# First attention: probabilities turned in place by VectorE in 32x32 blocks, values on every partition group, product in 32x32 tiles

## The chip, the cores and the metric

The kernel runs on one core of one Trainium2 chip. The core has five engines with instruction streams of their own: TensorE (matrix products; PE in the profile, its weight loads PEld), VectorE (DVE), ScalarE (ACT), GpSimd (POOL) and SyncE (SP), which here issues most of the DMAs. The metric is the device time of one execution in microseconds (us); lower is better.

## The reference, cut to what matters

There are 8 sequences (batches) of 128 tokens with 512 features, all in 32-bit floats. A transformer block is computed in two halves:

```python
x = x + attn1(einsum('bsi,boi->bso', x, lora_weight[adapter]))   # the first attention
x = x + ffn(attn2(x))                                            # the second stage
# attn1: 32 query heads of 16 features, 8 key/value heads, each shared by 4 query heads
scores = einsum('bihd,bjhd->bhij', q, k) * 16 ** -0.5
scores = where(causal, scores, finfo.min)
attn = softmax(scores)                     # [b, 32 heads, 128 queries, 128 keys]
out = einsum('bhij,bjhd->bihd', attn, v)   # then out @ wo
```

The change is in `attn1`, in the step from `attn` to `out`. The second stage (an attention over a paged cache with 32 heads of 128 features, its projections and a feed-forward layer with LoRA terms) is not touched.

## The kernel before

Everything is issued by hand in one order; each engine works through its own instructions in that order, and semaphores make it wait for the others.

The first attention fills roughly the first 205 us of the span, and the merging of LoRA weights runs beside its end. Its main loop runs over steps `k = 0..16`. Steps `2b` and `2b+1` belong to batch `b`; `hb = k % 2` selects half of its 32 heads, namely 16 heads, which lie as 4 row groups `j` of 32 partitions, 2 query repeats `rr` and 2 halves `half` (a head has 16 features, so that two heads share the 32 rows of a group, and zeros fill the other half). Step 16 has only left-over work. A step does the following:

- `scores1(k)` (L574 on): TensorE adds the causal mask (16 bf16 products in tiles of 32 rows, L583) and the scores (8 products of 32 rows by 256 columns, L595) into two PSUM tiles `sc` of 8 heads each. VectorE takes the negated maxima `nm` (L604), two instructions.
- `exps1(k, n)` (L613): ScalarE computes 8 exponentials for each of the two PSUM tiles, into an SBUF tile `pr` of 128 queries x 8 heads x 128 keys.
- `divide1(k, n)` (L623): VectorE sums (L627) and takes reciprocals (L628), GpSimd multiplies (L629).
- In the step after, `flip_p(last, j, copy)` (L633), for the four groups `j`: TensorE turns four 128x128 blocks of `pr` against the identity (L638), and VectorE or ScalarE copies the result from PSUM to an SBUF tile `pT` (L644). Keys then lie on the partitions.
- At the end of that step, `values1(last)` (L649): 8 products, 128 keys by 32 rows of output each (L657), and one copy by VectorE into `oT` (L664).

Beside this a step does its share of the projections of the next batch. An even step holds `flip_x1` (a finished batch turned for the second stage, x1Tp, L499), `condition(b+1)` (the LoRA layer, hp, L514, copied to `hT` by VectorE), `project_k` and `project_v` (kvp, L545 and L552), `keep_k` and `keep_v` (L556, L563; ScalarE copies; the values go to `vpad`, which has the zeros). An odd step holds `out_proj1(b-1)` (att, L673, added to the input by VectorE as `x1`, L677, and written to DRAM by SP), `project_q(b+1)` (qp, L530, copied to `qT` by VectorE, L540), `flip_x(b+2)` (xTp, L499) and `load_x`. The next even step's scores need `qT`.

Some steps hold extra work. Step 1 ends with `indices` (four VectorE instructions for `idx_kv`), steps 3 and 5 with `tables` (GpSimd), steps 3 and 7 issue the loads of second-stage weights on SP, step 9 issues `merge_loads` on SP (its last ones, `las` and `lbs`, wait for buffers that `condition(7)` frees in step 12). Step 12 ends with `merge_gates` (five VectorE instructions), step 13 with the gathers `kg` and `vg` (GpSimd), step 14 has `merge_a` (four products aeff and four VectorE copies `a_eff`, L464), step 15 has the first query and key products of the second stage with `q_turn`, `kv_turn` and `norms` (VectorE, ScalarE and GpSimd in turn), step 16 `queries(0)`, `merge_b` (beff) and `merge_w` (weff). After the loop come `keys(0)`, `own_keys(0)` and two more `merge_w`.

PSUM has three pools of two buffers each. `tp` serves everything that is turned, `mm` the projections and, before, the value products, `sc` the scores. In SBUF, `pr` has four buffers and `pT` five.

The second stage turns its own probabilities by VectorE in 32x32 blocks (L883) and moves the blocks by DMA; it is mentioned here since its rows in the profile show that instruction.

## Time and profile before

| | |
|---|---|
| median of 3 runs | 1414.29 us (1413.98 to 1414.86) |
| the profiled execution's own time | 1423.96 us |
| its span (first to last instruction) | 1421.1 us, mean granted TensorE clock 0.997 |
| TensorE (PE) busy | 1391.5 us, 98% of the span |
| VectorE (DVE) busy | 931.8 us, 66% |
| ScalarE (ACT) busy | 655.9 us, 46% |
| GpSimd (POOL) busy | 568.2 us, 40% |

The profile is of one execution. The page has the busy time of each engine, the groups of instructions by line with their count, busy time and mean duration, and the chain of waits that ended last. The trace behind it answers for stretches of the span: windows with the busy time of each engine, and a timeline in order of time. A line of the timeline has the start, the time taken, the engine, the line of the kernel, the operation, the tiles (out<-in), the shapes and how many instructions are merged; a bracket at its end tells how long the engine had been idle before it and which instruction ended that. A 32-bit matrix product appears as two records (two passes over its columns), one that turns a block or works in bf16 as one. Ends of matrix products are modelled, so the distance between starts is the better measure of what one costs.

In the windows one batch of the first attention in the middle takes 21.8 us.

### The profile page before, as it was taken

What the parts mean: (1) busy time and instruction counts of PE and PEld (TensorE: products, weight loads), DVE (VectorE), ACT (ScalarE), POOL (GpSimd) and SP (SyncE); (2) the same over time, 40 slices, a digit from 0 to 9 for tenths busy, and PEclk for the clock granted to TensorE, in tenths of its full rate; (3) what the DMA queues carried; (4) which work ended last, traced back from release to release, by engine and by line L of the source; (5) the groups of instructions that cost most, each with busy time, mean ns of one, the idle gap of its engine ahead of it and who ended that gap; (6) DMA issues with size and microseconds to landing.
All of it is one profiled execution on the core that took longest, in us unless ns stands there. A gap on an engine that the chain in (4) does not pass through costs nothing.

```text
span 1421.1 us, 20290 instructions
## 1 busy us (share of the span) xinstructions
PE 1391.5 (98%) x6244; PEld 898.5 (63%) x6244; DVE 931.8 (66%) x2266; ACT 655.9 (46%) x1520; POOL 568.2 (40%) x553
## 2 busy tenths in 40 slices
PE   6999989999999999999999999999999999999998
PEld 6877755566666666666666666666666665666555
DVE  5777846566666666666666666666666665666651
ACT  3555535444444444444444444444444444344431
POOL 5774342433333333333333333333333433343220
PEclk9999999999999999999999999999999999999999
DMA  6255013444444565444445654444456544444440
GB/s 198 75 164 183 31 37 104 129 117 118 119 115 119 161 193 151 119 119 119 119 119 159 196 148 119 118 119 119 121 160 192 152 117 136 131 111 112 115 111 30
DMA packets 156202, 180.26 MB, mean 127 GB/s; under 512 B 92416, under 2 KB 97792, under 8 KB 156096
## 3 DMA queue, kind: packets, MB, share of 16 engines
q1 hardware_dynamic: 140544, 134.39, 34.0%
q0 software_dynamic: 15552, 44.58, 10.8%
q8 instruction: 50, 0.82, 0.2%
q14 instruction: 56, 0.46, 0.1%
HBM read 75.83 MB, written 4.72 MB: 57 GB/s over the span
## 4 chain that ended last, share of the span: by engine, by line
PE 93%; DVE 2%; issue 2%; DMA 1%; ACT 1%; POOL 1%; SPq 1%; another core or an unknown queue 0%; DVEq 0%; POOLq 0%; ACTq 0%
PE op L963 19%; PE qp L177 15%; PE sc L889 15%; PE yp L982 15%; PE kvp L217 7%; PE sc L896 4%; PE fp L1044 2%; PE hp L514 2%; PE qTp L254 2%; PE pT1p L638 2%; PE qp L530 2%; PE att L673 2%; PE o L657 1%; PE sc L595 1%; PE kvp L545 1%
## 5 line engine op out<-in xcount | busy, mean ns | idle before, releaser
L902 DVE CUSTOM_DVE_ANT_0 pr<-sc,mask,nq 128x640 f32<-128x640 f32 x256 | 226.0, 884 | 144.2 <-PE sc L896 90.9
L912 ACT ACTIVATE pr<-pr,nm 128x640 f32<-128x640 f32 x256 | 211.8, 827 | 189.3 <-DVE nm L902 102.1
L889 PE MATMUL sc<-kT,qT 128*128 128x512 f32 x512 | 262.0, 593 | 0.0
L177 PE MATMUL qp<-wq,x1T 128*128 128x512 f32 x512 | 251.2, 593 | 0.0
L963 PE MATMUL op<-pT,vg 128*128 128x256 f32 x1024 | 242.0, 379 | 1.6 <-DMA pT<-fl 1.6
L203 POOL TENSOR_TENSOR qa<-qa,qb 128x512 f32<-128x512 f32 x64 | 81.8, 1278 | 375.2 <-DVE sums L879 375.2
L982 PE MATMUL yp<-wo,oT 128*128 128x512 f32 x504 | 229.2, 598 | 2.0 <-DVE oT L971 2.0
L963 PEld LDWEIGHTS op<-pT,vg 128*128 128x128 f32 x1024 | 193.9, 190 | 27.8 <-DVE sums L879 1.8
L880 ACT ACTIVATE pr<-pr,sums 128x640 f32<-128x640 f32 x256 | 208.4, 814 | 0.0
L883 DVE STREAM_TRANSPOSE fl<-pr 128x640 f32<-128x640 f32 x252 | 189.2, 808 | 0.0
L896 PEld LDWEIGHTS sc<-kTo,qT 128*128 128x128 f32 x512 | 96.4, 190 | 124.4 <-issue 119.2
L982 PEld LDWEIGHTS yp<-wo,oT 128*128 128x128 f32 x504 | 91.4, 191 | 95.1 <-issue 91.5
L160 POOL DMA_INDIRECT kg<-in_k_cache_dram,idx_kv x128 | 131.6, 1029 | 35.3 <-issue 34.8
L160 POOL DMA_INDIRECT vg<-in_v_cache_dram,idx_kv x128 | 128.6, 1005 | 37.8 <-issue 33.6
L889 PEld LDWEIGHTS sc<-kT,qT 128*128 128x128 f32 x512 | 87.7, 191 | 80.2 <-issue 77.8
L256 ACT COPY qT<-qTp 128x512 f32<-128x512 f32 x64 | 37.5, 586 | 205.3 <-PE qTp L254 204.7
L217 PEld LDWEIGHTS kvp<-wkv,x1T 128*128 128x128 f32 x512 | 97.3, 190 | 40.5 <-issue 30.1
L217 PE MATMUL kvp<-wkv,x1T 128*128 128x256 f32 x512 | 121.0, 379 | 0.0
L244 POOL TENSOR_TENSOR rs<-ss,minus_half 128x5 f32<-128x5 f32 x64 | 76.5, 1196 | 83.1 <-DVE ss L242 82.2
L177 PEld LDWEIGHTS qp<-wq,x1T 128*128 128x128 f32 x512 | 82.8, 191 | 31.5 <-issue 31.5
L896 PE MATMUL sc<-kTo,qT 128*128 128x128 f32 x512 | 99.2, 275 | 0.0
L273 ACT COPY kTo<-kTp 128x128 f32<-128x128 f32 x64 | 17.1, 267 | 166.4 <-issue 115.2
(155 smaller groups left out, 1701.1 us busy)
## 6 DMA issues: line engine op xcount, KB each, us to landing
pT<-fl SPq DMA_DIRECT2D x1008, 80.0 KB
kT<-flk SPq DMA_DIRECT2D x480, 32.0 KB
wq<-in_wq_dram SPq DMA_DIRECT2D x8, 1024.0 KB
wo<-in_wo_dram SPq DMA_DIRECT2D x8, 1024.0 KB
wkv<-in_wkv_dram SPq DMA_DIRECT2D x8, 512.0 KB
kg<-in_k_cache_dram,idx_kv POOLq DMA_INDIRECT x128
vg<-in_v_cache_dram,idx_kv POOLq DMA_INDIRECT x128
res<-x_kept SPq DMA_DIRECT2D x8, 256.0 KB
```

Source lines behind the costliest of these rows:

```text
L160: nc.gpsimd.indirect_dma_start(out=dst[:, c].rearrange("p n d -> p (n d)"), out_offset=None, in_=src, in_offset=bass.IndirectOffsetOnAxis( ...
L177: nc.tensor.matmul(s["qp"][:].rearrange("p h d -> p (h d)"), x1T[b][:, c, :], weights[g][0][:, c, :], start=(c == 0), stop=(c == KC - 1),)
L203: nc.gpsimd.tensor_tensor(qa[:], qa[:], qb[:], ALU.add)
L217: nc.tensor.matmul(s["kp"][:], x1T[b][:, c, :], weights[g][1][:, c, :], start=(c == 0), stop=(c == KC - 1))
L880: nc.scalar.activation(prs[r][:], prs[r][:], AF.Copy, scale=sums[:, r : r + 1])
L883: nc.vector.transpose(s["flips"][:, :, :, r, :].rearrange("p b c j -> p c b j"), prs[r][:])
L889: nc.tensor.matmul(sc[:, : NBLK * P].rearrange("p (k j) -> p k j", j=32), s["qT"][:, r, :], s["kT"], start=True, stop=True,)
L896: nc.tensor.matmul(sc[:, NBLK * P : NK], s["qT"][:, r, :], s["kTo"][:], start=True, stop=True)
L902: nc.vector.tensor_tensor_reduce(out=pr[:], in0=sc[:, :NK], in1=mask[:], scale=s["nq"][:, r : r + 1], scalar=3.0e38, op0=ALU.add, op1=ALU.min,
L912: nc.scalar.activation(pr[:], pr[:], AF.Exp, bias=nm[:, r : r + 1], scale=-1.0, accum_out=sums[:, r : r + 1],)
L963: nc.tensor.matmul(ops[h][:, : 2 * S], cached(u, "vg", c) if c < NBLK else s["vo"][:], s["pT"][:, :, c, 2 * h : 2 * h + 2, :].rearrange("p ...
L982: nc.tensor.matmul(yp[:], s["oT"][:, r, :], weights[g][2][:, r, :], start=(r == 0), stop=(r == REP - 1))
```

## The change

The probabilities are no longer turned by TensorE. `turn1(last)`, called directly after `scores1(k)`, lets VectorE transpose each 32x32 block of both probability tiles in place. So block `k` of 32 keys of a query group `a` ends on partitions `32a..32a+31`, where the queries of the group were. For the product the values of every key block must lie on every partition group: `keep_v` writes `vpad` to DRAM once and reads it back into `vrep`, four times, once for each partition group. `values1(b, groups)` then works per batch in place of per step: 32x32 tiles of the array at row group `a` (queries' group) and column group `j`, 128 columns (2 steps x 2 repeats x 32 queries), summed over key blocks `0..a` and halves; blocks above the diagonal are zeros and are left out. Groups 1 and 0 take 24 products, groups 3 and 2 take 56. Both calls are in the even step after the batch, ahead of and behind `project_k`; the two PSUM tiles of a call are the two `tp` buffers, and each is copied by VectorE into its 32 columns of `oT`. `divide1(k, 1)` of an even step moves behind the second call. The tiles `pr` of a batch's two steps become halves of one tile per `n`, with two buffers each; `x1` has one buffer where it had two.

```diff
@@ -387,8 +387,8 @@
 
         def angles():
 
-            fr = p1.tile([P, B, D2 // 2], F32, tag="pT", name="ang_f", bufs=5)
-            kf = p1.tile([P, B, D2 // 2], F32, tag="pT", name="ang_k", bufs=5)
+            fr = p1.tile([P, B, D2 // 2], F32, tag="pr1_0", name="ang_f")
+            kf = p1.tile([P, B, D2 // 2], F32, tag="pr1_1", name="ang_k")
 
             for n, key in enumerate(("sin", "cos")):
                 trig[key] = x1T[B - 1 - n][:].rearrange("p c (h d) -> p (c h) d", d=HALF)
@@ -560,11 +560,23 @@
                     kbd[b][:, half, :], ps[:, 0, :], AF.Copy, scale=odd[:, half : half + 1]
                 )
 
+        vrep = {}
+
         def keep_v(b, ps):
+
+
             for half in range(2):
                 nc.scalar.copy(
                     vpad[b % 2][:, :, half, half, :],
                     ps[:, 1, :].rearrange("p (j h d) -> p j h d", h=2, d=HD1)[:, :, half, :],
+                )
+            kept = dram.tile([P, 4 * 2 * 32], F32, tag="v1", name=f"v1_kept_{b}", bufs=2)
+            nc.sync.dma_start(out=kept[:], in_=vpad[b % 2][:].rearrange("p j h s d -> p (j h s d)"))
+            vrep[b] = p1.tile([P, 4, 4 * 2 * 32], F32, tag="vrep", name=f"vrep_{b}")
+            for a in range(4):
+                nc.sync.dma_start(
+                    out=vrep[b][32 * a : 32 * a + 32],
+                    in_=kept[:].rearrange("(k c) x -> c k x", c=32),
                 )
 
 
@@ -608,62 +620,70 @@
                     ALU.max,
                     negate=True,
                 )
-            h["pr"] = []
+
+
+
+        prs = {}
 
         def exps1(k, n):
             h = H[k]
-            pr = p1.tile([P, 8, S], F32, tag="pr1", name=f"pr1_{k}_{n}", bufs=4)
+            b, hb = divmod(k, 2)
+            if hb == 0:
+                prs[b, n] = p1.tile([P, 2, 8, S], F32, tag=f"pr1_{n}", name=f"pr1_{b}_{n}")
             sc = h["sc"][n][:].rearrange("p j (h t) -> p (j h) t", t=S)
             for m in range(8):
                 nc.scalar.activation(
-                    pr[:, m, :], sc[:, m, :], AF.Exp, bias=h["nm"][:, n, m : m + 1]
-                )
-            h["pr"].append(pr)
+                    prs[b, n][:, hb, m, :], sc[:, m, :], AF.Exp, bias=h["nm"][:, n, m : m + 1]
+                )
 
         def divide1(k, n):
-            h = H[k]
+            b, hb = divmod(k, 2)
             sums = p1.tile([P, 8], F32, tag="sums1", name=f"sums1_{k}_{n}", bufs=4)
-            pr = h["pr"][n]
-            nc.vector.tensor_reduce(sums[:], pr[:], AX.X, ALU.add)
+            pr = prs[b, n][:, hb]
+            nc.vector.tensor_reduce(sums[:], pr, AX.X, ALU.add)
             nc.vector.reciprocal(sums[:], sums[:])
             nc.gpsimd.tensor_tensor(
-                pr[:], pr[:], sums[:].unsqueeze(2).to_broadcast([P, 8, S]), ALU.mult
-            )
-
-        def flip_p(k, j, copy):
...
+        def turn1(k):
+
+
+            b, hb = divmod(k, 2)
+            for n in range(2):
+                pr = prs[b, n][:, hb].rearrange("p m t -> p (m t)")
+                nc.vector.transpose(pr, pr)
+
+        oT = {}
+
+        def values1(b, groups):
+
+            if b not in oT:
+                oT[b] = p1.tile([P, REP, S], F32, tag="oT1", name=f"oT1_{b}") if b + 1 < B else oT_kept
+            ps = {a: p_tp.tile([P, REP, S], F32, tag="tp", name=f"o1_{b}_{a}") for a in groups}
+            for block in range(4):
                 for half in range(2):
...
+                    for j in range(4):
+                        for a in groups:
+                            if block > a:
+                                continue
+                            rows = slice(32 * a, 32 * a + 32)
+                            nc.tensor.matmul(
+                                ps[a][32 * j : 32 * j + 32, 0, :].rearrange(
+                                    "p (h r i) -> p h r i", h=2, r=2
+                                ),
+                                vrep[b][rows, block, 64 * j + 32 * half : 64 * j + 32 * half + 32],
+                                prs[b, j // 2][rows].rearrange(
+                                    "p h (j r x) (k i) -> p h j r x k i", j=2, r=2, i=32
+                                )[:, :, j % 2, :, half, block, :],
+                                start=(block == 0 and half == 0),
+                                stop=(block == a and half == 1),
+                            )
+            for a in groups:
+                nc.vector.tensor_copy(
+                    oT[b][:, :, 32 * a : 32 * a + 32],
+                    ps[a][:, 0, :].rearrange("p (r i) -> p r i", i=32),
+                )
 
         x1 = {}
 
@@ -673,15 +693,13 @@
                 nc.tensor.matmul(
                     ps[:], oT[b][:, r, :], wo_sb[:, r, :], start=(r == 0), stop=(r == REP - 1)
                 )
-            x1[b] = p1.tile([P, DM], F32, tag="x1", name=f"x1_{b}")
+            x1[b] = p1.tile([P, DM], F32, tag="x1", name=f"x1_{b}", bufs=1)
             nc.vector.tensor_tensor(x1[b][:], ps[:], xss[b][:], ALU.add)
             nc.sync.dma_start(out=x1_kept[b][:], in_=x1[b][:])
 
         def flip_x1(b):
             tp = transposed(x1[b], f"x1Tp_{b}")
             nc.scalar.copy(x1T[b][:], tp[:])
-
-        by_vector, by_scalar = nc.vector.tensor_copy, nc.scalar.copy
 
         flip_x(0)
         turns = angles()
@@ -703,6 +721,8 @@
             more, now, last = b + 1 < B, k < 2 * B, k - 1
             if now:
                 scores1(k)
+            if k:
+                turn1(last)
             if hb == 0:
                 if b >= 2:
                     flip_x1(b - 2)
@@ -718,18 +738,17 @@
                 if k == 2 * B:
                     queries(0)
                 if k:
-                    flip_p(last, 0, by_vector)
-                    flip_p(last, 1, by_vector)
+                    values1(b - 1, (1, 0))
                 if now:
                     divide1(k, 0)
-                    divide1(k, 1)
                 if more:
                     kv = project_k(b + 1)
                 if k == 2 * B:
                     merge_b(0)
                 if k:
-                    flip_p(last, 2, by_scalar)
-                    flip_p(last, 3, by_scalar)
+                    values1(b - 1, (3, 2))
+                if now:
+                    divide1(k, 1)
                 if more:
                     project_v(b + 1, kv)
                     keep_k(b + 1, kv)
@@ -737,8 +756,6 @@
                     merge_b(1)
                     for i in range(2):
                         merge_w(i)
-                if k:
-                    values1(last)
                 if more:
                     keep_v(b + 1, kv)
                 gather_w(b + 3)
@@ -749,8 +766,6 @@
                     out_proj1(b - 1)
                 exps1(k, 0)
                 exps1(k, 1)
-                flip_p(last, 0, by_vector)
-                flip_p(last, 1, by_vector)
                 divide1(k, 0)
                 divide1(k, 1)
                 if more:
@@ -763,8 +778,6 @@
                         part()
                     for c in range(KC):
                         kv_matmul(0, c)
-                flip_p(last, 2, by_scalar)
-                flip_p(last, 3, by_vector)
                 if more:
                     project_q(b + 1, ps, (REP - 1,))
                     keep_q(b + 1, ps)
@@ -773,7 +786,6 @@
                     norms(0)
                 if b + 2 < B:
                     flip_x(b + 2)
-                values1(last)
                 load_x(b + 4)
                 if b == 0:
                     indices()
```

More of the change, by code (lines that the diff above doesn't have):

```diff
@@ L628, in divide1 @@
+            nc.vector.tensor_reduce(sums[:], pr, AX.X, ALU.add)
             nc.vector.reciprocal(sums[:], sums[:])
             nc.gpsimd.tensor_tensor(
-                pr[:], pr[:], sums[:].unsqueeze(2).to_broadcast([P, 8, S]), ALU.mult
+                pr, pr, sums[:].unsqueeze(2).to_broadcast([P, 8, S]), ALU.mult
             )
-        def flip_p(k, j, copy):
-            h = H[k]
-            tp = p_tp.tile([P, 2, 2, S], F32, tag="tp", name=f"pT1p_{k}_{j}")
-            for rr in range(2):
-                for half in range(2):
-                    nc.tensor.transpose(
-                        tp[:, half, rr, :],
-                        h["pr"][j // 2][:, j % 2 * 4 + 2 * rr + half, :],
-                        ident[:],
-                    )
-            pT = p1.tile([P, 2, 2 * S], F32, tag="pT", name=f"pT1_{k}_{j}", bufs=5)
-            copy(pT[:], tp[:].rearrange("p h r t -> p h (r t)"))
-            h[f"pT_{j}"] = pT
@@ L647, in block_kernel @@
-        oT = {}
-        def values1(k):
-            b, hb = divmod(k, 2)
-            h = H[k]
-            if hb == 0:
-                oT[b] = p1.tile([P, REP, S], F32, tag="oT1", name=f"oT1_{b}") if b + 1 < B else oT_kept
-            ps = p_mm.tile([P, 2 * S], F32, tag="mm", name=f"o1_{k}")
-            for half in range(2):
-                for j in range(4):
-                    nc.tensor.matmul(
-                        ps[32 * j : 32 * j + 32, :],
-                        vpad[b % 2][:, j, half].rearrange("p s d -> p (s d)"),
-                        h[f"pT_{j}"][:, half, :],
-                        start=(half == 0),
-                        stop=(half == 1),
-                    )
-            nc.vector.tensor_copy(
-                oT[b][:, 2 * hb : 2 * hb + 2, :].rearrange("p r t -> p (r t)"), ps[:]
-            )
+        def turn1(k):
[3 more added lines that the diff above has]
+                nc.vector.transpose(pr, pr)
```

## Prediction

> **What bounds the kernel now.** The page comes first, to see which engine fills the span; then the windows of single batches, because the change touches only the first 220 us; then the chain of waits inside one batch; then the order of VectorE's instructions in it.
>
> ```profile
> PE 1391.5 (98%) x6244; PEld 898.5 (63%) x6244; DVE 931.8 (66%) x2266; ACT 655.9 (46%) x1520; POOL 568.2 (40%) x553
> ```
> ```profile
> 107.10:128.90 21.80, 21.80 (x232) 17.49 (x236) 15.85 (x22) 12.38 (x41) 11.38 (x9) 1.00 0.28 91
> 173.20:220.60 47.40, 43.33 (x258) 25.85 (x257) 23.19 (x41) 15.73 (x48) 19.39 (x18) 0.96 0.14 45
> ```
> The second column is the stretch, the next are busy PE, PEld, DVE, ACT, POOL. A batch of the first attention is two steps and 21.8 us long; TensorE is busy for all of it, VectorE for 15.85. The chain agrees; these are its first pieces in an even step:
>
> ```profile
> 107.10 0.34 PE sc L583 x16
> 107.43 0.92 PE sc L595 x16
> 108.35 0.59 PE x1Tp L499 x4
> 108.94 3.57 PE hp L514 x32
> 112.51 0.87 PE pT1p L638 x8
> 113.38 1.07 PE kvp L545 x8
> ```
> Then come another pT1p of 0.87, kvp 0.89 and o 1.00. The odd step adds att 3.63, two more pT1p of 0.87, qp 2.68 and 0.89, xTp 0.44, o 1.00. So this stage is TensorE alone, and TensorE time taken out of it is worth its full length until another engine's chain is longer.
>
> ```profile
> 108.40 2.36 DVE L604 TENSOR_REDUCE nm<-sc 128x8 f32<-128x1024 f32 x2 [0.81 <-PE sc L595]
> 112.55 0.69 DVE L522 COPY hT<-hp 128x512 f32<-128x512 f32 x1 [1.80 <-PE hp L514]
> 113.16 1.28 DVE L644 COPY pT<-pT1p 128x512 f32<-128x512 f32 x2
> 114.35 1.21 DVE L627 TENSOR_REDUCE sums<-pr 128x8 f32<-128x1024 f32 x1
> 115.59 0.20 DVE L628 RECIPROCAL sums<-sums 128x8 f32<-128x8 f32 x1
> 115.72 1.19 DVE L627 TENSOR_REDUCE sums<-pr 128x8 f32<-128x1024 f32 x1
> ```
> VectorE waits in its order for TensorE (brackets). What counts on a full VectorE is the distance between starts: 1.14 for nm, 0.61 for hT, x or a pT copy, 1.24 + 0.13 for a sum with its reciprocal.
>
> **TensorE, per batch.** Removed: four groups of turns, 4 x 0.87, and two products, 2 x 1.00: 5.48 us. Added: 80 products of 32x32 with 128 columns, each in two passes. Nothing in the trace has 32 rows and 32 columns at once; its neighbours have one of them:
>
> ```profile
> 149.56 1.07 PE L657 MATMUL o<-pT,vpad 128*32 128x256 f32 x16
> 150.56 0.40 PE L583 MATMUL sc<-eye,causal 32*128 32x128 bf16 x16
> 150.80 1.09 PE L595 MATMUL sc<-kbd,qT 32*128 32x256 f32 x16
> ```
> Single records show that the four column groups of o start 7 ns apart and then every 0.216 us for 256 columns; the four row groups of sc do the same, 3 to 4 ns apart. So a pass of 128 columns takes 0.108 and four tiles run at once. Groups 1 and 0 need four rounds (the busier row group has 2 blocks x 2 halves), groups 3 and 2 eight; a round is 0.216 if all eight tiles of it run at once: 0.86 and 1.73, with 0.1 of drain each as after o (the next starts 0.31 after o's last start, its pass being 0.216): 0.99 and 1.83, in all 2.82. Bounds: only four tiles at once gives 24/4 x 0.216 and 56/4 x 0.216, in all 4.5; one at a time 80 x 0.216 = 17.3. I take 2.82, nearest to rows in which four rows and four columns were each fully parallel and neither read a partition more often than now. TensorE alone would then need 21.76 - 5.48 + 2.82 = 19.10.
>
> Starts set no limit in this: the 16 causal passes lie in 0.40 us with the last 0.21 long, so 12 ns apart, and a round of eight tiles has 14 ns for each. [...]
>
> **VectorE, per batch.** Removed: five pT copies (0.67) and two oT copies (0.42): 4.2 us. Added: four turns of 128x1024. Nearest rows:
>
> ```profile
> L883 DVE STREAM_TRANSPOSE fl<-pr 128x640 f32<-128x640 f32 x40 | 30.1, 808 | 0.0
> L840 DVE STREAM_TRANSPOSE flk<-kg 128x256 f32<-128x256 f32 x16 | 5.7, 412 | 0.2
> ```
> The slope is 1.03 ns an element, so 1.20 us each, 1.13 from start to start (0.727 and 0.326 in the records). And four copies of 128 elements: 0.42 at 256 and 0.67 at 512 give 0.29 each, 0.22 apart. Added 6.0; VectorE becomes 17.6 us busy. ScalarE loses three copies of 0.59, which lay in idle time: nothing.
>
> The cost is where these stand. turn1 is first behind the nm of the next step, so x1, hT, the sums and the next qT all queue behind it. One batch, from the end of a qT copy (0.00), in start times:
> - sc follows, and nm starts at 1.31 (24.22 to 25.53 at the first step). Turns 3.59 and 4.72, ended 5.93; GpSimd's divisions ended near 2. hT 5.85.
> - TensorE, done with hp at 5.4, waits for the second turn: values(1,0) 6.01 to 7.00; its two copies end at 7.64, sum and reciprocal 7.57 to 8.93.
> - kvp 7.00 to 8.07, values(3,2) 8.07 to 9.90 (both PSUM banks free at 7.64), kvp 10.80, sc 12.06. Copies 10.05 to 10.5, second sum 10.48 to 11.9.
> - Odd step: nm 12.17, turns 14.45 and 15.58 (GpSimd's second division ended at 14.0), x1 16.7 (att ended 15.7), sums 17.3 and 18.67 (ScalarE's exps ended 15.8 and 17.9), qT 20.03 to 20.72. TensorE had qp at 19.3 and waits.
>
> So the batch takes 20.72 instead of 21.76, and VectorE's order ends it: of 2.66 us saved on TensorE 1.04 remain.
>
> **The stage.** The first pair has no values; its odd step gets two turns and loses copies, and nm of the second batch moves from 44.29 to 43.1 (idx_kv, 1.8 us of VectorE, stands before it). Five batches at 20.72 bring nm of batch 6 to 146.7, where it was 151.93. There merge_gates (3.3 us of VectorE, at 161.16) delays the odd step's nm; the 0.6 that VectorE now idles there hides little of it, so this batch takes 23.7 against 22.6. Batch 7's nm: 170.4 against 174.54.
>
> The tail has a stall that I can't explain:
>
> ```profile
> 184.07 0.42 DVE L464 COPY a_eff<-aeff 128x256 f32<-128x256 f32 x1 [3.85 <-PE pT1p L638]
> 185.57 0.42 DVE L464 COPY a_eff<-aeff 128x256 f32<-128x256 f32 x1 [1.08 <-remote]
> 186.74 1.16 PE L638 MATMUL pT1p<-ident,pr 128*128 128x128 f32 x8 [3.60 <-DVE pT L644]
> ```
> TensorE loses 3.6 us here. Walked in the same way without it, the last turn ends 30 us behind nm, then values 0.99, beff 3.44, values 1.83, beff 3.44, weff 1.91, kgTp and kTp 0.7, weff 1.91: 44.3 us from nm to the second stage, against 46.1 before. With the stall values(1,0) stands in its place and 1.7 of it are left: 46.0. I keep the stall. The stage then ends 4.1 to 5.9 us sooner; I take 4.3. What follows is TensorE's own and moves with it.
>
> DMAs: five more per batch on SP's queue, some 0.4 us each to issue, four of them behind the landing of the first. Behind them queue x1_kept, load_x and the weights. The values are wanted 30 us after they are copied, so they cost nothing. The tightest is merge_loads, which held SP until 155.41: behind it now stand the copies of batch 6 and then x1_kept of batch 4, which the single x1 buffer wants landed before the addition of batch 5 at about 165; the queue is through at about 161. If that cover fails, VectorE stops by the difference.
>
> **Sum.** The profiled execution took 1423.96 us, its span 1421.1; the median of the runs is 1414.29, 9.67 below. 4.3 off: 1419.7 for an execution under the profiler, 1410.0 for the median. What can be told from no change is 0.2%, 2.8 us.
>
> **Rivals.**
> - Slower: the array runs only four of these tiles at once. For it: no row has more than four. Against: rows and columns were each free of each other. Both products lie on the chain above (turn, values, kvp, values, sc, nm), so 1.7 more a batch, over seven batches 12: 1422. It loses time from 0.6 us more per batch on.
> - Slower: the halves of one pr tile are ordered as a whole, so that the odd step's exps wait for the turn: they end at 21.1 instead of 17.9, the batch takes 23.2, six times 2.5: 1425. Against it: the exps at 109.72 began while the second nm still wrote its half of one tile.
> - Faster: VectorE's order costs less than I walk, down to TensorE's 19.10 a batch: six times 1.6 more, 1400. Against it: VectorE's own starts sum to 17 and each batch must wait 1.3 for sc.
> - The values arrive late from DRAM: in the stretch of the table DMA is busy for 0.28, against it.
>
> **Chances.** Forecast 0.66 (of it 0.45 faster, 0.17 same, 0.04 slower, for half a microsecond per batch in a walk of twenty links is 3 us), four tiles 0.20, exps 0.06, faster rival 0.05, late values 0.03. Faster 0.50, same 0.17, slower 0.33. The range 1404 to 1423 takes in the forecast with and without the stall and the four-tile case.
>
> **What would show it.** Right: passes of o1 eight at a time in rounds of 0.216; turns of 1.20 us; TensorE idle before values (about 0.6) and before sc at even steps (about 1, released by qT); batches of 20.7; ScalarE 1.8 less busy a batch. Wrong: batches above 21.8, values(3,2) over 2.5 us, exps released by a turn, or x1 released by a DMA.

## The result and the profile after

The changed kernel takes 1423.16 us (median of six runs, 1421.67 to 1426.64) where the kernel before takes 1414.63 in the same measurement: 1.0064 times, 95% interval 1.0051 to 1.0077. It is 8.5 us slower; the forecast was 1410.0, 4.3 faster, with a range up to 1423. The profiled execution took 1425.54 us, its span 1423.8.

The first line of the page: TensorE has 768 more matmul records and 7.6 us less busy time, VectorE 13 us more.

```profile
PE 1383.9 (97%) x7012; PEld 893.8 (63%) x7012; DVE 945.2 (66%) x2274; ACT 641.3 (45%) x1496; POOL 567.8 (40%) x553
```

The windows of one regular batch, from nm to nm, and of the tail, from the nm of step 14 to the first scores of the second stage (columns as before; after POOL stand the granted clock, the DMA share and GB/s):

```profile
109.13:129.98 20.85, 20.07 (x321) 16.07 (x322) 17.23 (x23) 10.47 (x38) 11.37 (x9) 1.00 0.38 116
175.40:224.63 49.23, 43.00 (x450) 25.79 (x450) 26.34 (x44) 12.96 (x43) 18.64 (x17) 0.85 0.13 44
```

The regular batch is what was forecast: 20.85 us instead of 21.77. The tail is not: 49.23 instead of 46.1, and the granted clock, 0.96 in the tail's line of before, is 0.85. The chain of waits through the even step shows the new order:

```profile
109.13 2.35 DVE nm L616 x2
111.48 2.29 DVE pr L655 x2
113.77 0.04 issue
113.81 1.07 PE o L671 x40
114.88 1.09 PE kvp L545 x8
115.97 1.94 PE o L671 x112
117.91 1.09 PE kvp L552 x8
119.00 0.33 PE sc L595 x16
```

The chain now runs through VectorE (nm and both turns), then through the value products; in the odd step it goes nm, turns, x, sums, qT. VectorE's own groups:

```profile
L655 DVE STREAM_TRANSPOSE pr<-pr 128x1024 f32<-128x1024 f32 x32 | 37.8, 1218 | 0.0
L683 DVE COPY oT<-o 128x128 f32<-128x128 f32 x28 | 6.8, 286 | 13.6 <-PE o L671 13.6
```

What TensorE waited for between 20 and 230 us (us in total, times, longest). In the kernel before such waits add up to 8 us, here to 20:

```profile
PE sc L607 <- DVE qT L540: 5.7, 7, 2.6
PE o L671 <- issue: 4.0, 2, 2.5
PE qTp L254 <- POOL qa L203: 3.0, 1, 3.0
PE sc L595 <- ACT pr L635: 2.2, 2, 1.2
PE o L671 <- DVE pr L655: 2.0, 7, 0.6
PE sc L607 <- DVE iota_sf L377: 2.0, 1, 2.0
```

The two largest of the kernel before, in the same stretch:

```profile
PE pT1p L638 <- DVE pT L644: 3.6, 1, 3.6
PE sc L595 <- DVE qT L540: 1.8, 1, 1.8
```

The timeline of TensorE at the last step shows the second half of the loss. It idles 3.01 us for qa and 2.52 for the last turn, which stands behind the key's rotation and the norms on VectorE (the trace names no engine for the second of them; that turn began at 203.30); and then the first group of b_eff takes 6.14 us, the second 3.70, with the same eight passes:

```profile
201.46 0.66 PE L254 MATMUL qTp<-ident,qa 128*128 128x128 f32 x4 [3.01 <-POOL qa L203]
204.63 0.77 PE L671 MATMUL o<-pr,vrep 32*32 32x128 f32 x8 [2.52 <-issue]
205.71 1.93 PE L671 MATMUL o<-pr,vrep 32*32 32x128 f32 x40 [0.31 <-DVE pr L655]
207.57 6.14 PE L469 MATMUL beff<-lb,gs 128*128 128x512 f32 x8
213.64 2.01 PE L671 MATMUL o<-pr,vrep 32*32 32x128 f32 x112
215.58 3.70 PE L469 MATMUL beff<-lb,gs 128*128 128x512 f32 x8
219.21 1.98 PE L484 MATMUL weff<-lbs,las 32*128 32x512 f32 x4
221.82 2.88 PE L484 MATMUL weff<-lbs,las 32*128 32x512 f32 x4
```

The granted clock is 0.50 in stretches that are multiples of 3.413 us: at 41.85 (one), 96.47 (one), 171.56 (two), 202.28 (three) and 222.76 us (two), nine windows or 30.7 us. The kernel before had two of one window each before 300 us (188.21 and 273.54). So the question was what makes the clock fall.

### The profile page after: what moved, and what is told of

Its sections match the earlier page's. It is cut to its first block, busy times and chain, and to the rows that moved or that the text cites. A ratio compares the mean times of both kernels' runs of the same rounds, so it can differ in the third digit from the quotient of the medians.

```text
span 1423.8 us, 21814 instructions
## 1 busy us (share of the span) xinstructions
PE 1383.9 (97%) x7012; PEld 893.8 (63%) x7012; DVE 945.2 (66%) x2274; ACT 641.3 (45%) x1496; POOL 567.8 (40%) x553
## 3 DMA queue, kind: packets, MB, share of 16 engines
q0 software_dynamic: 15552, 44.58, 10.7%
## 4 chain that ended last, share of the span: by engine, by line
PE 87%; DVE 8%; issue 2%; POOL 1%; DMA 1%; SPq 1%; ACT 0%; DVEq 0%; POOLq 0%
PE op L975 19%; PE sc L901 15%; PE qp L177 15%; PE yp L994 15%; PE kvp L217 7%; PE sc L908 4%; DVE pr L655 2%; DVE nm L616 2%; PE fp L1056 2%; PE qTp L254 2%; PE o L671 2%; DVE sums L643 1%; PE sc L607 1%; PE beff L469 1%; PE kvp L545 1%
## 5 line engine op out<-in xcount | busy, mean ns | idle before, releaser
L217 PEld LDWEIGHTS kvp<-wkv,x1T 128*128 128x128 f32 x512 | 97.5, 190 | 40.3 <-issue 30.3
```

The costliest lines, as they stand in the source:

```text
L217: nc.tensor.matmul(s["kp"][:], x1T[b][:, c, :], weights[g][1][:, c, :], start=(c == 0), stop=(c == KC - 1))
```

## The experiments

Stage lengths, from the nm starts (step 14 is batch 7's even step) and the first scores of the first two units of the second stage, in us:

| run | five batches (steps 2 to 12) | steps 12 to 14 | 14 to second stage | first unit | time against before |
|---|---|---|---|---|---|
| before, as in the page | 107.64 | 22.61 | 46.08 | 16.15 | |
| e1 (before) | 107.61 | 22.61 | 45.59 | 16.15 | 0.9997 |
| after, first profile | 107.30 | 24.56 | 49.23 | 18.58 | 1.0064 |
| e5 (after) | 105.94 | 23.62 | 52.85 | 16.15 | 1.0067 |
| e3 | 107.32 | 21.75 | 55.90 | 18.23 | 1.0082 |
| e11 | 106.93 | 24.56 | 47.92 | 16.16 | 1.0023 |
| e16 | 107.86 | 20.25 | 53.25 | 16.15 | 1.0033 |
| e8 | 107.23 | 20.26 | 45.44 | 16.15 | 0.9935 |
| e12 | 103.49 | 20.25 | 43.92 | 16.16 | 0.9946 |
| e13 (before) | 107.63 | 22.61 | 41.26 | 16.19 | 0.996 |
| e14 | 106.79 | 23.94 | 49.40 | 16.19 | 1.0046 |
| e15 | 103.65 | 20.26 | 47.95 | 18.40 | 0.998 |
| e17 | 105.10 | 20.26 | 39.95 | 17.49 | 0.9932 |

The kernel before takes 1414 us on one chip and 1422 on another, so times are compared as ratios to it on the same chip.

**e1: the kernel before again.** 

> The kernel before, unchanged, profiled once more. Question: do the stalls of its first profile (3.6 us of TensorE idle at 183.14 and 2.0 at 270.44, each followed by a window of 3.41 us with a granted clock of 0.50, about 9 us in all; that execution took 1423.96 us against a median of 1414.29) belong to the kernel or to that one execution? Theory A (they belong to that execution): median 1414, the new profile's own time within 3 us of it, no idle of TensorE over 2.5 us between 100 and 300 us, granted clock 0.998 or more. Rival (they belong to the kernel, and the profiler lengthens every execution by some 9 us): the same idle times at the same places, profiled execution near 1424.

Measured: 0.9997 of the other runs of before (0.9988 to 1.0007); the profiled execution 1421.36 us, the median of its runs 1420.8. Half for each theory. The stall at 183 us recurs, 3.39 us long with a half-clock window behind it, so it belongs to the kernel. The wait of 2.0 us at 270 is 0.92 this time, without a half-clock window, and the profiled execution lies 0.6 above its median, not 9.7. So that distance, which the forecast carried over, belonged to one execution.

**e2: TensorE's waits filled with work.** 

> The changed kernel with work added: products of 128x128 by 128x512 whose result nobody reads stand on TensorE where it waits in the changed kernel: one ahead of the scores of steps 2 and 14, two between their mask and their product with qT, three ahead of queries(0) and two behind it at the last step (11 in all, 0.87 us each, 9.5 us more TensorE work, within idle times of 1.22 + 1.96, 0.99 + 2.56 and 3.01 + 2.52 us). Theory A (TensorE's waits for VectorE cost twice: the wait, and then half clock for one or more windows of 3.41 us): the windows of clock 0.50 at 41.85, 171.56 and 202.28 go, the b_eff product at the last step takes 3.6 us instead of 6.1, and the time falls by 4 to 8 us, to 1415 to 1419, though TensorE does more. Rival B (the loss is in the small products themselves, or in VectorE's longer chain alone; the low clock is no cost): the time stays at 1423 or rises by up to 3 us.

```diff
+            if k in (2, 14): fill(f"fill_a_{k}", 1)      # ahead of the mask
...
+            if k in (2, 14): fill(f"fill_b_{k}", 2)      # ahead of qT's product
...
+                    fill("fill_q", 3)
                     queries(0)
+                    fill("fill_v", 2)
```

Measured: 1.0115 (1.0092 to 1.0139). Wrong. The half-clock windows behind the filled waits are gone in the profile, but half clock comes at two other places, 189.87 and 224.00, for 6.8 us each, and in the four executions the mean clock is 0.986 to 0.995 (the profile is of the fastest of them). The window ahead of the second, 220.59 to 224.00, is 0.85 filled with passes, the end of b_eff and w_eff among them. "Waits make the clock fall" does not cover these windows.

**e3: qT copied by ScalarE.** 

> The changed kernel with one edit: the scaled copy of qp to qT (0.64 to 0.69 us, last in VectorE's order of an odd step) is made by ScalarE. Theory A (VectorE's order ends each batch, at qT): qT no longer waits for the turns and sums; a batch falls from 20.86 to about 20.0 between the nm starts, the waits of TensorE for qT at steps 2 and 14 (1.96 and 2.56 us) and the half-clock windows behind them go; 7 x 0.8 + 3 to 5: 1413 to 1416. Rival B (TensorE's small products set the batch): the batch stays at 20.8, and only the waits at steps 2 and 14 change: 1419 to 1423.

```diff
-            nc.vector.tensor_scalar(qT[b][:], ps[:], SCALE1, None, ALU.mult)
+            nc.scalar.activation(qT[b][:], ps[:], AF.Copy, scale=SCALE1)
```

Measured: 1.0082 (1.0063 to 1.0101). The regular batches fall to 20.5 us, less than half of what was expected; steps 12 to 14 take 21.75. All of it is lost: at step 2 TensorE, now early, waits 3.48 us for the turn, and half clock follows for 10.2 us; the tail takes 55.9 us, with ten more us at half clock behind step 14's values.

**e4: the b_eff products first.** 

> The changed kernel with one edit: at the last step (16) the two b_eff products (3.44 us each at full clock), which wait for nothing there, stand before and behind queries(0), ahead of the first values instead of between and behind them. Theory A (TensorE idles 3.0 + 2.5 us there for qa and for turn1(15), which stands behind the rotation and the norms on VectorE, and then runs at half clock for 10.2 us): the idle time falls from 5.5 to about 1.5, the three cold windows at 202 go, the second stage starts 6 to 9 us sooner: 1414 to 1417. Rival B (what ends the stage lies elsewhere, for instance in the keys or the gathered pages): the second stage starts as before, 1421 to 1424.

```diff
                 if k == 2 * B:
+                    merge_b(0)
                     queries(0)
+                    merge_b(1)
```

Measured: 1.0032 (1.0016 to 1.0048). The idle of the last step is gone and the second stage starts 46.84 us behind nm; but half clock now comes at 216.32 for 10.2 us, where both value products and w_eff stand next to each other. The gain is less than expected; that this half clock is the reason is read from the profile, not tested.

At this point the windows of the clock were compared with the passes in them. A pass counts its columns times 0.84 ns (the 0.216 us per 256 columns of the prediction; half of it for bf16, whose 16 passes of 128 columns in four row groups start within 0.19 us, every 0.056 us in a group) times the share of the 128 rows that it uses; four column groups at once count as one; passes at half clock count as at full clock. It was first done with cells, rows times columns.

**e5: the changed kernel again.** 

> The changed kernel, unchanged, once more, as the base for the next three on this chip and to see which of its lost times recur. Theory C: a window of 3.41 us in which TensorE's products cover less than about a third of the array's time (share of the 128 x 128 cells times time) is followed by a window at half clock; products in tiles of 32x32, eight at a time, count for about 0.3 however busy TensorE looks, and the 32-row w_eff products for 0.25. By it the half-clock windows behind step 14's and 16's adjacent values and behind w_eff (223 us) recur, the single idle of 1.48 us before a value product at 94 us needn't; 1.004 to 1.008 of the kernel before. Rival B (they are accidents of one execution): other places, clock over 0.995, within 0.2% of the kernel before.

Measured: 1.0067 (1.0041 to 1.0093). Half-clock windows recur at 42.09, 175.22, 188.87 and 209.35, not at 96 and 223; 188.87, behind step 14's values, is new. Steps 2, 14 and 16 hold them in both profiles. That the phase of the windows decides which place is hit is a reading, not a test.

**e6 and e7: the same extra time on TensorE, with all of the array and with one tile.** 

> The kernel before with work added that nobody reads: six products of 128x128 with 512 columns (0.87 us each) ahead of the scores of steps 4, 6, 8 and 10; 24 in all, 20.9 us of TensorE. Both theories: +19 to +22 us, no window of half clock in these batches. It is the base for the next run.

> As e6_more_full, but each of the 24 products uses 32 rows and 32 columns of the array instead of 128 and 128: the same number of instructions, columns and passes, TensorE as busy as there (5.2 us at each of four places), one sixteenth of the cells. Theory C (the clock goes by the share of the array at work, not by TensorE being busy): a window of clock 0.50 at each of the four places, one or two long, +7 to +14 us against e6. Rival (the clock falls only where TensorE is idle): the same time as e6, within 2 us, and no half-clock window there.

```diff
+            if k in (4, 6, 8, 10):
+                t = p_tp.tile([P, DM], F32, tag="tp", name=f"more_{k}")
+                for i in range(6):                       # e6; e7: t[0:32], 32 rows, 32 columns
+                    nc.tensor.matmul(t[:], wk_sb[:, 0, :], wq_sb[:, 0, :], start=True, stop=True)
             if now:
                 scores1(k)
```

Measured: e6 1.0147 (1.0130 to 1.0164), 1444.0 us; e7 1.0223 (1.0206 to 1.0241), 1454.13: 10.1 us more for the same number of passes and columns. The windows of e7 around the second place (PE busy is the second number, the clock the third from the end):

```profile
90.82:94.23 3.41, 3.41 (x19) 0.77 (x10) 0.42 (x1) 0.11 (x1) 3.41 (x4) 1.00 0.99 341
94.23:97.64 3.41, 3.41 (x5) 0.67 (x4) 0.00 (x0) 0.00 (x0) 3.41 (x3) 0.50 0.87 305
97.64:101.05 3.41, 3.41 (x34) 1.55 (x32) 0.00 (x0) 0.00 (x0) 0.53 (x2) 0.50 0.12 44
```

For comparison, a window of e6 in its second place, filled with full products:

```profile
92.38:95.79 3.41, 3.41 (x9) 1.52 (x8) 0.00 (x0) 0.00 (x0) 3.41 (x4) 1.00 0.97 327
```

TensorE is busy through all of these, and in e7 alone the clock halves. So in these runs the clock went by how much of the array the products use, not by whether TensorE had work. At step 4 of e7, though, it stayed at 1.00, against theory C, which counts cells.

**e9 and e10: a quarter and half of the columns, all rows.** 

> As e6_more_full (the kernel before with 24 more products, six at each of four places, 20.9 us), but each product uses 128 rows and 32 columns, one quarter of the array. Theory C (below about a third of the array's cells over 3.41 us the clock halves): half-clock windows at most of the four places, +5 to +12 us against e6's 1.0147, so 1.018 to 1.023 of the kernel before. Rival (only products of one row group, or idle time, lower the clock): 1.0147, no such windows.

> The same with 64 columns, one half of the array. Theory C: above a third, so no half-clock window at the four places and the time of e6_more_full, 1.013 to 1.0165 of the kernel before. Rival (any product narrower than the array lowers the clock): +5 us or more against it.

```diff
-                    nc.tensor.matmul(t[:], wk_sb[:, 0, :], ...
+                    nc.tensor.matmul(t[:32], wk_sb[:, 0, :32], ...    # e9; e10: 64
```

Measured: e9 1.0144 (1.0124 to 1.0164), e10 1.0143 (1.0126 to 1.0161): both as e6, no half-clock window at the four places. e9 was expected to be slow. The windows of e9 at the second place, which are filled from 91.61 to 96.92 with products of 128 rows and 32 columns:

```profile
90.41:93.82 3.41, 3.41 (x26) 1.28 (x25) 1.10 (x2) 0.59 (x1) 3.41 (x3) 1.00 1.05 381
93.82:97.23 3.41, 3.41 (x28) 0.98 (x30) 0.00 (x0) 0.00 (x0) 3.41 (x4) 1.00 1.02 372
```

So with 32 columns each the clock fell in e7, with 32 rows, and not in e9, with 128: here rows counted. By rows, the shares at e7's step 4 are 0.38 and 0.41. Over the 1482 windows between 16 and 290 us of all nineteen profiles (in those of before and after, 158 windows, 11 lie below 0.34 and all are followed by half clock, and none of the 147 others is):

| share of rows in the window | windows | next one at half clock |
|---|---|---|
| below 0.34 | 77 | 77 |
| 0.34 to 0.37 | 13 | 7 |
| 0.37 to 0.40 | 12 | 0 |
| above 0.40 | 1380 | 0 |

**e8: waits and thin stretches taken out.** 

> The changed kernel with the waits and the thin stretches taken out: qT and hT copied by ScalarE, the page indices computed before the first qT, the gate products by GpSimd, step 14's values between the a_eff products, the last step's values between the b_eff products, the last turn ahead of the key's rotation. Nothing else is moved and the attention's own products are those of the changed kernel. Theory (the small products and the turns are cheaper, as predicted, and what is lost is waits for VectorE and half-clock windows behind thin stretches): a batch of 19.6 to 20.5 us, at most three half-clock windows before 230 us, the second stage starts 8 to 13 us sooner than in the changed kernel; 0.992 to 0.997 of the kernel before. Rival (the products themselves are the loss): batches of 20.8, 1.003 or more.

```diff
-            nc.vector.tensor_scalar(qT[b][:], ps[:], SCALE1, None, ALU.mult)
+            nc.scalar.activation(qT[b][:], ps[:], AF.Copy, scale=SCALE1)
...
-            (nc.vector.tensor_copy if b else nc.scalar.copy)(hT[b][:], hp[:])
+            nc.scalar.copy(hT[b][:], hp[:])
...
+        indices()                                  # ahead of the first qT, not at step 1
         ps = new_q(0)
...
-                nc.vector.tensor_tensor(
+                nc.gpsimd.tensor_tensor(
                     merge["gs"][c].rearrange("p (b r) -> p b r", r=RANK),
...
# step 14:  merge_a(0), merge_a(1), values (1, 0), merge_a(2), merge_a(3), values (3, 2)
# step 15:  q_turn, turn1(15), kv_turn, norms
# step 16:  merge_b(0), queries, values (1, 0), merge_w(0), merge_b(1), merge_w(1),
#           values (3, 2), merge_w(2), keys, own_keys, merge_w(3)
```

Measured: 0.9935 (0.9917 to 0.9952), 1414.2 against 1422.24: 8 us faster than before and 16 faster than the changed kernel (e5, 1430.07), with its attention products and turns unchanged. Steps 6 to 12 take 20.56 a batch. The second stage starts 188.94 us behind the first nm (before: 194.6 in e1), although half clock still took 10.2 us from 47.05 on and the batch there 25.0. Not all of this belongs to the attention's products: 2.75 of the 5.6 us at that point lie between the first two batches' nm (16.01 us against 18.76 in e1), where the page indices stood. The kernel before was never given these moves.

**e11 and e16: e8 in two halves.** 

> The changed kernel with only the order of steps 14 to 16 of e8_rearranged: step 14's values between the a_eff products, the last step's between the b_eff products, the last turn ahead of the key's rotation. VectorE keeps the copies of qT and hT, the page indices and the gates. Theory (the loss of the changed kernel sits in the tail: 52.9 and 49.2 us from the nm of batch 7 to the second stage, where the kernel before has 45.6 and 46.1): the tail takes 44 to 47 us, 1.000 to 1.004 of the kernel before against 1.0067. Rival (the loss sits in the batches, and the copies moved to ScalarE were what helped): 1.006 or more.

> The complement of e11_order_only: the changed kernel with VectorE relieved (qT and hT copied by ScalarE, the page indices before the first qT, the gates by GpSimd) and the order of steps 14 to 16 as in the changed kernel. Theory (waits for VectorE in steps 2 to 14 and thin stretches in the tail are two separate losses that add): e8 has 1.32% less than the changed kernel, e11 0.44%, so 0.88% less here: 0.996 to 1.000 of the kernel before; batches of 20.5 us; the tail from nm 14 to the second stage still 49 us or more. Rival (the relief helps only together with the order): 1.004 or more.

Measured: e11 (the order alone) 1.0023 (1.0013 to 1.0033), tail 47.92; e16 (VectorE's relief alone) 1.0033 (1.0021 to 1.0044), where 0.996 to 1.000 was expected. Against 1.0067 the halves bring 0.44% and 0.34%, together 1.32%: they do not add. In e16 TensorE reaches the tail sooner and waits there for what the tail's order sets: 1.79 and 2.52 us idle at the last step, and half clock at 184.46 and 204.94 for 6.8 us each. At step 2 half clock takes 10.2 us (from 47.93), as in e8.

**e12: e8 with more work.** 

> e8_rearranged with three products of 128x128 by 128x512 added that nobody reads (0.87 us each): two ahead of step 2's first values, one ahead of the last step's, both in places where TensorE waits 1.4 and 0.4 us and which were followed by three and one windows of half clock. Theory C: adding 2.6 us of TensorE work takes away the three windows at 47 us (about 4.5 us of time) and the one at 204 us (1.7): 0.988 to 0.992 of the kernel before, against 0.9935. Rival (the low clock there has another cause): 0.9935 to 0.995.

```diff
+                if k in (2, 2 * B):
+                    fill(f"fill_{k}", 2 if k == 2 else 1)
                 if k:
                     values1(b - 1, (1, 0))
```

Measured: 0.9946 (0.9927 to 0.9965): no gain over e8 that these runs can tell. In the profiles it does what was expected. Two windows of e8 and then two of e12 at the same place:

```profile
43.64:47.05 3.41, 1.98 (x41) 1.52 (x45) 3.07 (x3) 3.41 (x14) 1.03 (x1) 1.00 0.02 6
47.05:50.46 3.41, 3.41 (x56) 2.78 (x41) 1.82 (x4) 1.06 (x5) 0.00 (x0) 0.50 0.03 5
```
```profile
44.00:47.41 3.41, 3.41 (x35) 2.14 (x41) 3.20 (x3) 3.41 (x14) 1.18 (x1) 1.00 0.02 7
47.41:50.82 3.41, 3.41 (x153) 3.09 (x142) 1.82 (x4) 1.20 (x5) 0.45 (x1) 1.00 0.02 5
```

Filled, the wait of 1.4 us is no longer followed by half clock, and this batch takes 20.55 instead of 24.98. But the windows do not lie at the same time in each execution (the edges here are at 47.05 in e8 and 47.41 in e12, at 41.85 in the first profile of the changed kernel and 42.09 in e5, by no multiple of 3.413 us apart): in two of e8's four executions the mean clock is 0.996, against 0.993 and 0.994 in the others, so e8 does not pay for it every time, and e12 pays elsewhere in some (0.993 in the slowest of its six).

**e13, e14, e15: the page gathers moved.** 

> The kernel before with one edit: the eight gathers of the first key and value pages, which GpSimd issues from 176 to 185 us (step 14), are issued behind the norms of the last step, at about 200 us. Theory D (the stall of 3.4 to 3.9 us of TensorE at 183 to 187, seen in every profile of the kernel before and its variants, comes from these gathers): no idle over 2 us there, no half-clock window at 189; from the nm of step 14 to that of step 15 about 14 us instead of 17.4; if the gathers hold up whatever runs beside them, a stall of the same size appears at 200 to 215. 0.996 to 1.000 of the kernel before. Rival (the stall belongs to the transposes and copies of that step): it stays, 1.000.

> The same edit in the changed kernel. Theory D: in step 14 the first 48 passes of the values, which start with pauses of 0.3 to 1.0 us and take 3 to 6 us there against 1.07 in other batches, take 1.1 to 1.5; from nm 14 to nm 15 it is 14 to 16 us instead of 19.4 (14.4 in the first profile); the last step's values may suffer instead. 1.002 to 1.006 against 1.0067. Rival: the pauses stay, 1.006 to 1.007.

> The same edit in e12_more_work. Theory D: step 14 loses its pauses and the half-clock window at 173, the second stage starts 2 to 4 us sooner: 0.990 to 0.993. Rival: as e12_more_work, 0.9946.

```diff
                     norms(0)
+                    gather(0, "kg")
+                    gather(0, "vg")
...
-                elif b == B - 2:
-                    gather(0, "kg")
-                    gather(0, "vg")
```

Measured: e13 0.996 (0.9944 to 0.9976); e14 1.0046 (1.0032 to 1.0060); e15 0.998 (0.9971 to 0.9989), slower than e12. In the kernel before the stall goes with the gathers; its line of the waits in e1, and then in e13:

```profile
PE pT1p L638 <- DVE pT L644: 3.4, 1, 3.4
```
```profile
PE pT1p L638 <- DVE pT L644: 0.4, 1, 0.4
```

Steps 14 to 15 take 13.01 us instead of 17.35. In the changed kernel the same gathers can slow the starts of the value products. This is step 14 in e5, where 48 passes take 3.9 us, then in e14, and last in the first profile, where the passes have no pause although the gathers are still there:

```profile
184.21 0.78 PE L671 MATMUL o<-pr,vrep 32*32 32x128 f32 x31
186.00 0.41 PE L671 MATMUL o<-pr,vrep 32*32 32x128 f32 x4 [1.01 <-issue]
186.72 0.26 PE L671 MATMUL o<-pr,vrep 32*32 32x128 f32 x1 [0.32 <-issue]
187.44 0.63 PE L671 MATMUL o<-pr,vrep 32*32 32x128 f32 x12 [0.45 <-issue]
```
```profile
185.07 1.09 PE L671 MATMUL o<-pr,vrep 32*32 32x128 f32 x48
```
```profile
184.29 1.10 PE L671 MATMUL o<-pr,vrep 32*32 32x128 f32 x48
```

So the gathers don't do it in every execution: of the nine profiles of the changed kernel and its variants that have them there, eight have step 14's first 48 passes drawn out over 2.6 us or more. The stall of the kernel before is in all six profiles of it that have the gathers there. And the gathers are not the loss: with them moved in both kernels, on the same chip, the changed one is still 11.1 us slower (e14 1428.07, e13 1417.0).

In e15 step 14 has one wait of 0.33 us, but the gathers now run beside the last step's products, and pauses are there, the longest before w_eff, with 13.65 us of half clock behind them:

```profile
202.18 1.12 PE L484 MATMUL weff<-lbs,las 32*128 32x512 f32 x2 [2.32 <-issue]
204.29 0.42 PE L676 MATMUL o<-pr,vrep 32*32 32x128 f32 x4 [0.41 <-issue]
205.74 2.91 PE L676 MATMUL o<-pr,vrep 32*32 32x128 f32 x82 [1.03 <-issue]
```

**e17: the gathers beside long products.** 

> e12_more_work with the page gathers moved away from every small product: the key pages' four between the exponentials and the divisions of step 15 (beside the output, query and key products with 512 and 256 columns), the value pages' four at the start of the second stage. Theory D (the gathers slow TensorE where it runs many short instructions, and only there): step 14 to 15 takes 13 to 14 us as in e13 and e15, the last step 25 to 27 us as in e12, the second stage starts 3 to 4 us sooner than in e12: 0.990 to 0.993 of the kernel before. Rival (any place costs the same, as in e15): 0.9946 to 0.998.

Its edit: `gather(0, "kg")` stands behind step 15's exponentials, `gather(0, "vg")` behind the start of the second stage. Measured: 0.9932 (0.9907 to 0.9957). The second stage starts 180.32 us behind the first nm, 3.35 sooner than in e12 (183.67), as expected; the whole time can't be told from e8's and e12's. In its profile 1.3 us go at the second unit's start, and two half-clock windows come late (1095 and 1371 us), behind waits of 2.0 us; waits at these two places are in every profile, 1.3 to 3.0 us long.

## Why the prediction was wrong

**TensorE's products: right.** Eight tiles run at once: the passes of values (1,0) and (3,2) take 1.1 and 2.01 us (0.99 and 1.83 forecast; the 40 passes behind the second turn 1.07). That is 160 passes in 3.1 us, 19 ns each on average; the eight of the round at 113.82 start 6 to 10 ns apart, and each tile's next pass every 0.109 us from the second round on.

**VectorE's part and the walk of a batch: right.** Turns 1.218 us (1.20 forecast), copies 0.286 (0.29), the batch 20.85 (20.72) with VectorE's order on the chain and qT at its end. Of the listed wrong signs two came in the first profile, both in one batch: it took 23.89 us, and its values (3,2) 3.65, with a pause of 1.48 in them. No exps waits for a turn and no x1 for a DMA. The five DMAs a batch cost nothing that shows.

**The stage: wrong, in four terms.** By the second unit of the second stage the changed kernel is 6.44 us behind (243.21 against 236.77), where 4.3 ahead was forecast. The 10.7 between are, step by step: nm of batch 1 at 43.54 for 43.1 (0.4); five batches 107.30 for 103.6 (3.7: 0.13 each, and 3.0 in one, where TensorE paused 1.48 us before a value product at 94 us and ran at half clock from 96.47 on); the batch with the gates 24.56 for 23.7 (0.9); the tail 49.23 for 46.0 (3.2); the first unit 18.58 for the 16.15 of before (2.4). The last four hold half-clock windows.

The tail can be set piece by piece against the forecast's own walk without the stall (44.3; the stall, 1.7 more in the forecast, didn't come in this execution). The last turn ends 30.3 us behind nm, for 30. From there, by the starts, values take 1.86 us for 0.99, the first b_eff 6.07 for 3.44 and the last w_eff 2.81 for 1.91: 4.4 of the 4.9 us over the walk, all of it in half-clock windows. Half clock also holds the 2.4 of the first unit, which takes 16.15 in e5 and e11 where no such window stands, and what the 3.0 have beyond the pause, 1.6. That makes some 8.4 of the 10.7 us, an estimate from this one profile.

**The step that failed is "TensorE time is worth its full length".** The sum gave each pass the duration of full clock. The change replaces 5.48 us per batch that use all rows of the array by 3.1 us that use 0.30 and 0.38 of them, and TensorE then waits for VectorE. In a regular batch the share of rows in a window falls to 0.43 or 0.47 (134.01 and 113.53), and no half clock follows. Where w_eff stands next to other thin work (0.335 from 219.35 on), or at a wait (0.29, 0.30 and 0.13 at steps 2, 14 and 16, from 38.44, 168.15 and 198.87 on), it falls below 0.34, and the next 3.41 us go at a granted clock of 0.50: a wait is paid twice. In e14 the scores behind step 14's values, which stand next to each other, take 1.90 us, against 1.09 in the first profile, as at half clock. The sign was in the prediction's own line: 0.96 in the clock column of the tail, read over. None of the rivals was about the clock.

The half-clock stretches of the first profile are multiples of 3.413 us, and idle time does not explain them all. In e7 a window that is busy for all of its 3.41 us, behind the first 0.4 us with 32-row products alone (90.82 to 94.23), is followed by half clock, and in the changed kernel a window with 1.48 us of idle is (93.05 to 96.47).

**The stall in the tail: a term carried over without a cause.** e13 shows that in the kernel before the gathers make it. In the changed kernel they can hit the short value products and bring half clock behind them: 19.4 us from step 14 to 15 in e5, 14.6 without them in e14. But in the first profile it is 14.4 with them. The forecast kept 1.7 us for it, which was too much for one execution and too little for the other.

**The base of the sum.** The 9.67 us between the profiled execution and the median were taken over as if every profile had them. After has 2.4 and e1 0.6. The two profiles differ by only 1.58 us, the medians by 8.5: the profile of before was of a long execution, whose third unit took 2.78 us more than in e1.

**What is shown and what is argued.** Shown: in a regular batch the products and turns are a gain (20.85 us, and 20.56 in e8, against 21.77); the clock went with the rows at work (e6, e7, e9, e10; half clock behind all 77 windows below 0.34, behind none of 1392 above 0.37); the gathers make the stall of the kernel before (3.4 us in e1, 0.4 in e13). Argued from the windows, not separated by a run: how much of the 8.5 us is half clock and how much the waits themselves. Not tested: e8's moves in the kernel before. So e8's 0.65% is what the exchange and the moves bring together, and what the exchange brings alone over the whole kernel, once the waits are gone, is open. Still open too: by what way GpSimd's gathers hold up TensorE's starts, and what made the single pauses at 94 us (1.48 us in the first profile, 1.10 in e11, 0.5 to 0.7 in e2, e4 and e5).

## What to carry to other kernels

Count a TensorE product not only by its time but by the rows that it uses. In this kernel the small tiles were cheap where full products stand around them (160 passes in 3.1 us for 5.48, a batch of 20.85 us for 21.77), and dear next to each other, to other products of few rows, or to a wait (clock 0.50 for the next 3.41 us behind every window with a share of rows below 0.34). When a change moves the bound to another engine, price the waits that TensorE gets at more than their length (behind waits of 3.01 and 2.52 us the first b_eff took 6.14 us, the second 3.70), and read the clock column of every stretch before the sum is made. A stall without a cause is no constant: the same gathers cost 4 us beside transposes (steps 14 to 15 in 17.35 us, 13.01 in e13), nothing or up to 5 beside short products (14.4 in the first profile and 19.4 in e5, 14.6 in e14), and little beside long ones (in e17 the second stage starts 3.35 us sooner than in e12).

## What the hardware showed unexpectedly

- The granted clock of TensorE went by the share of the 128 rows that its passes used in windows of 3.413 us: below 0.34 all 77 windows were followed by half clock, above 0.37 none of 1392. Columns didn't count: products of 128 rows and 32 columns (e9) kept 1.00 at all four places, those of 32 rows and 32 columns (e7) fell to 0.50 from 94.23 on, though not at step 4.
- Adding 1.74 us of full products in front of a thin stretch shortened that batch by 4.43 us in the profile (20.55 in e12, 24.98 in e8).
- Beside indirect gathers issued by GpSimd, whose queue took 21% of the DMA engines' time in that stretch of e11, TensorE paused between short products for 0.3 to 1.0 us at a time (e5) and before w_eff for 2.3 us (e15), but not in every execution: the first profile of the changed kernel has no such pause.
- 32x32 tiles of different row and column groups started 19 ns apart on average (160 passes in 3.1 us), the nearest two 5 ns.
